# Edge rows scattered in columns of 124 rows instead of 128, with zero rows in pieces of many sizes

## The chip, the cores and the metric

The kernel runs on one core of a Trainium2 chip. The metric is the device time of one execution in microseconds (us). A core has five engines that run side by side: TensorE (PE; its weight loads are shown apart as PEld), VectorE (DVE), ScalarE (ACT), GpSimd (POOL) and SyncE (SP), and 16 DMA engines that move data between the DRAM (HBM) and the on-chip memory of 128 partitions.

## The reference

A graph layer. 206250 edges, sorted by destination, carry a row of 128 numbers each; the row of every edge is added to its source node (6250 nodes). The sums go with the node's features and a global row through a small MLP; the input is added back and each row is normed.

```python
edge_aggr = jnp.zeros((n, HIDDEN), dtype=x.dtype).at[row].add(edge_features)   # row = src
combined = jnp.concatenate([x, edge_aggr, global_expand], axis=-1) @ W_c + b_c
h = jax.nn.softplus(combined @ W1 + b1)
h = jax.nn.softplus(h @ W2 + b2)
return _layernorm(x + h @ W3 + b3)
```

## The kernel before, in words

The kernel first sorts the edge rows by their source node, in DRAM, and then sums what lies together. Nodes are taken in blocks of 128, so there are `NB` = 49 buckets. In the scratch tensor `bucketed` each bucket has room for a whole number of superchunks of 256 rows (`SC`; `NSC` = 854 in all). A row there has 129 numbers (516 bytes): the 128 of the edge and, last, the node's place in its block.

**Counting (lines 104 to 172).** The list of source nodes is laid out on 128 partitions: partition p holds the edges p x 1611 to p x 1611 + 1610 (`T` = 1611 columns), and one more column takes the 42 edges that are left (`R`), so `TC` = 1612. DVE turns node numbers into a bucket number (`block`) and a place within it (`low`), and then makes 49 passes over the columns (line 150), one for each bucket, which mark its edges (`in_block`) and count them. Two small matmuls and a scan give each bucket's start and each partition's first position (`base`).

**Zero rows (lines 174 to 190 and 216 to 218).** Behind the last edge of each bucket 256 zero rows are written, those that have no room there to a spare place behind all buckets. DVE works out the positions `pad_i`, and POOL writes them in two scatters of 128 rows for each bucket, 98 in all.

**Positions (lines 225 to 237).** In groups of 90 columns DVE runs, for each bucket, a scan (line 233) and a predicated copy (line 235), which give each edge its position; the group's positions become integers in `pos`.

**Row scatter (lines 239 to 253).** For each nine columns SP loads a tile `rows` (line 242) of 128 x 9 edge rows, ACT writes their `low` into the 129th place (line 245), and POOL issues nine indirect DMAs (line 210), one for each column, which send 128 rows each to the positions in that column of `pos`. The pool of `rows` has four buffers, and a load waits for the nine scatters that read its buffer last. POOL's queue holds the 98 zero scatters, then the 1612 row scatters, in this order; no two are held to be dependent on each other.

**Sums (lines 282 to 300).** When all scatters have landed, SP loads eight superchunks at a time (`chunks`); for each 128 rows DVE makes a one-hot matrix `hot` from the 129th number, TensorE multiplies it with the rows, and DVE adds the product to the block's part of `sums_t`.

**MLP (lines 321 to 362).** For 512 nodes at a time the three layers, the residual and the norm follow, and SP stores the rows.

Tile framework code puts in the waits; each engine works through its own queue in order.

## Time and profile before

| | us |
|---|---|
| time, median of two runs (3343.35 to 3343.64) | 3343.49 |
| span of the profiled execution, first to last instruction | 3156.7 |
| what lies around the span (median less span) | 186.8 |
| first scatter starts | 112.87 |
| first row scatter starts | 266.77 |
| last scatter starts, takes | 2319.15, 0.90 |
| first load of the sums issued | 2321.40 |

The profile is one execution; its span is the time between its first and its last instruction. The page gives no device time of its own for that execution, so the median of the runs stands for it, and the 186.8 us around the span are taken as fixed.

Busy time of the engines in the span: PE 716.9 us, PEld 527.9, DVE 1161.0, ACT 178.2, POOL 1695.3. A row of the groups names the line, the engine and the operation, what is written and read, how often, the busy time and mean length of one in ns, and the idle time of its engine just before it with what ended that idle time. "Issue" there means that the engine waited for nothing that the profile shows. Three more groups of the same page:

```profile
L233 DVE TENSOR_TENSOR_SCAN scan<-ones,scan,in_block 128x90 f32<-128x90 f32 (+1 forms) x833 | 323.1, 389 | 0.0
L235 DVE COPY_PREDICATED pos_f<-in_block,scan 128x90 f32<-128x90 uint8 (+1 forms) x882 | 200.0, 228 | 0.0
L150 DVE TENSOR_SCALAR_CACHE_REDUCE in_block<-block 128x1612 uint8<-128x1612 bf16 x49 | 85.9, 1821 | 0.0
```

The DMA issues give, after the count, the size of one and the median time from issue to landing:

```profile
rows<-in_edge_attr SPq DMA_DIRECT2D x179, 576.0 KB, 4.6
bucketed<-rows,pos POOLq DMA_INDIRECT x1612, 2.4
bucketed<-zeros,pad_i POOLq DMA_INDIRECT x98, 2.4
```

POOL's queue of DMAs (q0) shows 54720 packets and 113.01 MB, SP's queue (q1) 328812 packets and 228.93 MB.

### The profile page before, as it was taken

The numbers are of one execution on the slowest core, as the hardware profiler recorded it, in microseconds if no ns is written. First come the engines' busy times: TensorE is split into PE (matmuls) and PEld (weight loads), VectorE is DVE, ScalarE is ACT, GpSimd is POOL, SyncE is SP. The second block draws the span as 40 slices with busy tenths as digits, with TensorE's granted clock in tenths as the row PEclk, the third lists the DMA queues.
The fourth block names the chain that finished last, engine by engine and source line by source line (L and its number), as shares of the span: only waits on it lengthen the run. The fifth ranks groups of instructions, "written<-read, shape, count | busy, mean of one in ns | idle before, by whom it ended". The sixth has DMA issues, their size and how long they took to land. (4 is left out here: it accounts for less than half of the span.)

```text
span 3156.7 us, 18596 instructions
## 1 busy us (share of the span) xinstructions
PE 716.9 (23%) x3776; PEld 527.9 (17%) x3776; DVE 1161.0 (37%) x4793; ACT 178.2 (6%) x368; POOL 1695.3 (54%) x1720
## 2 busy tenths in 40 slices
PE   0000000000000000000000000000049999999885
PEld 0000000000000000000000000000037777777543
DVE  9999995000000000000000000000029999999644
ACT  0000000000000000000000000000000000000267
POOL 1577777777777777777777777777730000000000
PEclk9999999999999999999999999999999999999965
DMA  3012333333333333333333333333356565656200
GB/s 128 15 48 71 97 98 103 103 101 104 104 105 105 104 105 104 105 105 105 104 105 104 105 105 105 104 103 102 102 156 188 176 187 177 185 178 185 68 16 24
DMA packets 386717, 346.72 MB, mean 110 GB/s; under 512 B 33101, under 2 KB 355802, under 8 KB 386602
## 3 DMA queue, kind: packets, MB, share of 16 engines
q1 hardware_dynamic: 328812, 228.93, 25.8%
q0 software_dynamic: 54720, 113.01, 11.0%
q10 hardware_dynamic: 3070, 3.60, 0.4%
q14 instruction: 85, 0.70, 0.1%
q8 instruction: 30, 0.49, 0.1%
HBM read 222.83 MB, written 122.57 MB: 109 GB/s over the span
## 5 line engine op out<-in xcount | busy, mean ns | idle before, releaser
L210 POOL DMA_INDIRECT bucketed<-rows,pos x1612 | 1562.0, 969 | 491.6 <-issue 489.4
L297 PE MATMUL part<-hot,chunks 128*128 128x128 f32 x3416 | 569.9, 302 | 2273.1 <-DVE hot L295 2246.5
L295 DVE TENSOR_SCALAR hot<-iota_f,chunks 128x128 f32<-128x128 f32 x1708 | 406.7, 280 | 1818.5 <-DMA chunks<-bucketed 1812.8
L297 PEld LDWEIGHTS part<-hot,chunks 128*128 128x128 f32 x3416 | 448.2, 191 | 2394.1 <-issue 2213.6
L233 DVE TENSOR_TENSOR_SCAN scan<-ones,scan,in_block 128x90 f32<-128x90 f32 (+1 forms) x833 | 323.1, 389 | 0.0
L300 DVE TENSOR_TENSOR sums_t<-sums_t,part 128x128 f32 x854 | 245.4, 287 | 63.2 <-PE part L297 34.9
L235 DVE COPY_PREDICATED pos_f<-in_block,scan 128x90 f32<-128x90 uint8 (+1 forms) x882 | 200.0, 228 | 0.0
L210 POOL DMA_INDIRECT bucketed<-zeros,pad_i x98 | 124.0, 1266 | 132.5 <-DVE pos_f L235 103.3
L245 ACT COPY rows<-low 128x9 f32<-128x9 f32 x179 | 36.6, 206 | 2230.0 <-DMA bucketed<-rows,pos 2219.4
L150 DVE TENSOR_SCALAR_CACHE_REDUCE in_block<-block 128x1612 uint8<-128x1612 bf16 x49 | 85.9, 1821 | 0.0
L329 ACT ACTIVATE comb<-comb_ps,c_bias 128x512 f32<-128x512 f32 (+1 forms) x13 | 8.4, 646 | 617.4 <-PE comb_ps L326 617.4
L340 PE MATMUL y_ps<-w_sb,h 128*128 128x128 f32 (+1 forms) x98 | 33.2, 437 | 26.1 <-DVE h L313 25.6
L341 PE MATMUL y_ps<-b_row,ones 1*128 1x128 f32 (+1 forms) x98 | 35.6, 459 | 0.0
L340 PEld LDWEIGHTS y_ps<-w_sb,h 128*128 128x128 f32 (+1 forms) x98 | 24.6, 291 | 53.5 <-DVE h L313 36.4
L310 ACT ACT_TABLE_LOAD x26 | 33.4, 1283 | 0.5
L313 DVE TENSOR_TENSOR h<-h,away 128x512 f32<-128x512 f32 (+1 forms) x26 | 17.1, 656 | 37.5 <-ACT away L310 37.5
L318 PE MATMUL z_ps<-h,w_sb 128*128 128x512 f32 (+1 forms) x26 | 22.8, 976 | 9.3 <-DVE h L313 9.3
L154 PE MATMUL before_ps<-count,after 128*128 128x49 f32 x2 | 0.7, 432 | 106.7 <-DVE in_block L150 106.7
L342 DVE TENSOR_TENSOR y<-y_ps,x_sb 128x128 f32<-128x128 f32 (+1 forms) x49 | 13.8, 285 | 29.6 <-PE y_ps L341 29.6
L309 ACT ACT_TABLE_LOAD x19 | 24.4, 1283 | 0.3
L341 PEld LDWEIGHTS y_ps<-b_row,ones 1*128 1x128 f32 (+1 forms) x98 | 22.1, 279 | 9.9 <-issue 8.5
L312 DVE TENSOR_SCALAR h<-z_ps,cols 128x512 f32<-128x512 f32 (+1 forms) x26 | 18.2, 707 | 14.7 <-ACT away L308 14.7
(85 smaller groups left out, 284.8 us busy)
## 6 DMA issues: line engine op xcount, KB each, us to landing
chunks<-bucketed SPq DMA_DIRECT2D x106, 1032.0 KB, 5.3
rows<-in_edge_attr SPq DMA_DIRECT2D x179, 576.0 KB, 4.6
bucketed<-rows,pos POOLq DMA_INDIRECT x1612, 2.4
bucketed<-zeros SPq DMA_DIRECT2D x14, 451.5 KB, 8.7
out<-y SPq DMA_DIRECT2D x12, 256.0 KB, 2.2
bucketed<-zeros,pad_i POOLq DMA_INDIRECT x98, 2.4
src_i<-in_src SPq DMA_DIRECT2D x1, 805.5 KB
chunks<-bucketed SPq DMA_DIRECT2D x1, 774.0 KB
```

The lines of the kernel that those rows point to most:

```text
L150: nc.vector.tensor_scalar(in_block[:, b, :], block, float(b), None, op0=ALU.is_equal, op1=ALU.add, accum_out=count[:, b:b + 1])
L210: s = nc.gpsimd.indirect_dma_start(out=bucketed[:, :], out_offset=bass.IndirectOffsetOnAxis(ap=index, axis=0), in_=rows, in_offset=None)
L233: nc.vector.tensor_tensor_scan(scan[:, b, :n], ones[:, :n], in_block[:, b, g0:g1], first, op0=ALU.mult, op1=ALU.add)
L235: nc.vector.copy_predicated(pos_f[:, g0:g1], in_block[:, b, g0:g1], scan[:, b, :n])
L245: nc.scalar.copy(rows[:, :k, D:W], low[:, c0:c0 + k].unsqueeze(2))
L295: nc.vector.tensor_scalar(hot, iota_f, chunks[:, s, j, D:W], None, op0=ALU.is_equal)
L297: nc.tensor.matmul(part, chunks[:, s, j, :D], hot, start=(j == 0), stop=(j == SUB - 1))
L300: nc.vector.tensor_add(here, here, part)
L309: nc.scalar.activation(away[:, :w], away[:, :w], AF.Exp, scale=-1.0)
L310: nc.scalar.activation(away[:, :w], away[:, :w], AF.Ln, bias=ones[:, :1])
L340: nc.tensor.matmul(y_ps[:r, :], h2[:, q0:q0 + r], w_sb["w3"], start=True, stop=False)
L341: nc.tensor.matmul(y_ps[:r, :], ones[:1, :r], b3_row, start=False, stop=True)
```

## The change

The edges are laid out on `EP` = 124 partitions: `T` becomes 1663, `R` 38 and `TC` 1664. Every tile with an edge on each partition (`src_i`, `node`, `block`, `low`, `in_block`, `count`, `pos`, `scan`, `rows`) shrinks to 124 partitions, and a row scatter sends 124 rows. The load of a tile of nine columns is issued as two DMAs, of 112 and of 12 partitions. `rows` has three buffers instead of four.

The 256 zero rows behind a bucket are scattered in pieces whose sizes come from a table of eight entries, one after the other over the buckets. The pieces of a bucket lie a constant step apart, which POOL writes with one `iota` for each bucket. The positions take 8 columns for each bucket instead of 2, used or not, and `bucketed` has more spare rows. The rest of the diff removes comments.

```diff
+EP = 124
+PAD_SIZES = ((127, 127, 2), (122, 122, 12), (124, 124, 8), (112, 112, 32), (64,) * 4, (32,) * 8,
+             (128, 128), (96, 96, 64))
+PAD_MAX = 8
...
-    T, R = divmod(E, P)
+    T, R = divmod(E, EP)
...
-    bucketed = dram.tile([ROWS + NB * SUB * P, W], F32, name="bucketed")
+    bucketed = dram.tile([ROWS + NB * PAD_MAX * P, W], F32, name="bucketed")
...
-        rows_p = phase.enter_context(tc.tile_pool(name="rows", bufs=4))
+        rows_p = phase.enter_context(tc.tile_pool(name="rows", bufs=3))
...
-        in_block = keep.tile([P, NB, TC], U8, name="in_block")
+        in_block = keep.tile([EP, NB, TC], U8, name="in_block")
...
-        nc.gpsimd.iota(spare, pattern=[[SUB * P, NB], [P, SUB]], base=ROWS, channel_multiplier=1,
-                       allow_small_or_imprecise_dtypes=True)
+        nc.gpsimd.iota(spare, pattern=[[PAD_MAX * P, NB], [P, PAD_MAX]], base=ROWS,
+                       channel_multiplier=1, allow_small_or_imprecise_dtypes=True)
+        for b in range(NB):
+            size = PAD_SIZES[b % len(PAD_SIZES)][0]
+            nc.gpsimd.iota(pad_f[:, b, :], pattern=[[size, PAD_MAX]], base=0,
+                           channel_multiplier=1, allow_small_or_imprecise_dtypes=True)
         nc.vector.tensor_add(pad_end, start, total)
-        for k in range(SUB):
-            nc.vector.tensor_scalar(pad_f[:, :, k], pad_end, part_f, float(k * P),
-                                    op0=ALU.add, op1=ALU.add)
+        for k in range(PAD_MAX):
+            nc.vector.tensor_add(pad_f[:, :, k], pad_f[:, :, k], pad_end)
             nc.vector.scalar_tensor_tensor(over[:, :, k], end, float(SC), pad_f[:, :, k],
                                            op0=ALU.mult, op1=ALU.is_le)
...
         for b in range(NB):
-            for k in range(SUB):
-                scatter(zeros[:, :W], pad_i[:, b, k:k + 1])
+            for k, r in enumerate(PAD_SIZES[b % len(PAD_SIZES)]):
+                scatter(zeros[:r, :W], pad_i[:r, b, k:k + 1])
...
-                rows = rows_p.tile([P, LOAD_COLS, W], F32, name="rows")
-                nc.sync.dma_start(
-                    rows[:, :k, :D],
-                    edge_attr[:P * T, :].rearrange("(p t) d -> p t d", p=P)[:, c0:c0 + k, :])
+                rows = rows_p.tile([EP, LOAD_COLS, W], F32, name="rows")
+                of = edge_attr[:EP * T, :].rearrange("(p t) d -> p t d", p=EP)
+                for p0, p1 in ((0, 112), (112, EP)):
+                    nc.sync.dma_start(rows[p0:p1, :k, :D], of[p0:p1, c0:c0 + k, :])
```

More of the change, by code (lines that the diff above doesn't have):

```diff
@@ L100 @@
         scans = phase.enter_context(tc.tile_pool(name="scans", bufs=2))
-        rows_p = phase.enter_context(tc.tile_pool(name="rows", bufs=4))
+        rows_p = phase.enter_context(tc.tile_pool(name="rows", bufs=3))
         ps = phase.enter_context(tc.tile_pool(name="ps", bufs=1, space=PSUM))
-        src_i = keep.tile([P, TC], I32, name="src_i")
+        src_i = keep.tile([EP, TC], I32, name="src_i")
         if R:
             nc.vector.memset(src_i[:, T:TC], 0)
-        nc.sync.dma_start(src_i[:, :T], src[:P * T].rearrange("(p t) -> p t", p=P))
+        nc.sync.dma_start(src_i[:, :T], src[:EP * T].rearrange("(p t) -> p t", p=EP))
         if R:
-            nc.sync.dma_start(src_i[:R, T:TC], src[P * T:].rearrange("(p o) -> p o", o=1))
+            nc.sync.dma_start(src_i[:R, T:TC], src[EP * T:].rearrange("(p o) -> p o", o=1))
         ZR = 7
@@ L121 @@
             )
-        node = keep.tile([P, TC], F32, name="node", tag="t0")
-        wrap = keep.tile([P, TC], F32, name="wrap", tag="t1")
+        node = keep.tile([EP, TC], F32, name="node", tag="t0")
+        wrap = keep.tile([EP, TC], F32, name="wrap", tag="t1")
         nc.vector.tensor_copy(node, src_i)
@@ L131 @@
         nc.vector.tensor_add(src_i, node, wrap)
-        part_i = keep.tile([P, TC], I32, name="part_i", tag="t1")
-        block = keep.tile([P, TC], BF16, name="block")
+        part_i = keep.tile([EP, TC], I32, name="part_i", tag="t1")
+        block = keep.tile([EP, TC], BF16, name="block")
         nc.vector.tensor_scalar(part_i, src_i, 7, None, op0=ALU.arith_shift_right)
@@ L136 @@
         if R:
-            none = keep.tile([P, 1], F32, name="none")
-            nc.vector.tensor_scalar(none, part_f, R - 0.5, 128.0, op0=ALU.is_gt, op1=ALU.mult)
+            none = keep.tile([EP, 1], F32, name="none")
+            nc.vector.tensor_scalar(none, part_f[:EP], R - 0.5, 128.0, op0=ALU.is_gt, op1=ALU.mult)
             nc.vector.tensor_add(block[:, T:TC], block[:, T:TC], none)
-        low_i = keep.tile([P, TC], I32, name="low_i", tag="t0")
-        low = keep.tile([P, TC], F32, name="low")
+        low_i = keep.tile([EP, TC], I32, name="low_i", tag="t0")
+        low = keep.tile([EP, TC], F32, name="low")
         nc.vector.tensor_scalar(low_i, src_i, P - 1, None, op0=ALU.bitwise_and)
         nc.vector.tensor_copy(low, low_i)
-        in_block = keep.tile([P, NB, TC], U8, name="in_block")
-        count = keep.tile([P, NB], F32, name="count")
+        in_block = keep.tile([EP, NB, TC], U8, name="in_block")
+        count = keep.tile([EP, NB], F32, name="count")
         for b in range(NB):
@@ L153 @@
         before_ps = ps.tile([P, NB], F32, name="before_ps")
-        nc.tensor.matmul(before_ps, after, count, start=True, stop=True)
+        nc.tensor.matmul(before_ps, after[:EP, :], count, start=True, stop=True)
         total_ps = ps.tile([P, NB], F32, name="total_ps")
-        nc.tensor.matmul(total_ps, ones, count, start=True, stop=True)
+        nc.tensor.matmul(total_ps, ones[:EP, :], count, start=True, stop=True)
         total = keep.tile([P, NB], F32, name="total")
@@ L172 @@
         nc.vector.scalar_tensor_tensor(base, start, -1.0, before_ps, op0=ALU.add, op1=ALU.add)
-        pad_f = keep.tile([P, NB, SUB], F32, name="pad_f")
+        pad_f = keep.tile([P, NB, PAD_MAX], F32, name="pad_f")
         pad_end = keep.tile([P, NB], F32, name="pad_end")
-        over = keep.tile([P, NB, SUB], F32, name="over")
-        spare = keep.tile([P, NB, SUB], F32, name="spare")
-        pad_i = keep.tile([P, NB, SUB], I32, name="pad_i")
-        nc.gpsimd.iota(spare, pattern=[[SUB * P, NB], [P, SUB]], base=ROWS, channel_multiplier=1,
-                       allow_small_or_imprecise_dtypes=True)
+        over = keep.tile([P, NB, PAD_MAX], F32, name="over")
+        spare = keep.tile([P, NB, PAD_MAX], F32, name="spare")
+        pad_i = keep.tile([P, NB, PAD_MAX], I32, name="pad_i")
+        nc.gpsimd.iota(spare, pattern=[[PAD_MAX * P, NB], [P, PAD_MAX]], base=ROWS,
[4 more added lines that the diff above has]
+                           channel_multiplier=1, allow_small_or_imprecise_dtypes=True)
         nc.vector.tensor_add(pad_end, start, total)
-        for k in range(SUB):
-            nc.vector.tensor_scalar(pad_f[:, :, k], pad_end, part_f, float(k * P),
-                                    op0=ALU.add, op1=ALU.add)
+        for k in range(PAD_MAX):
+            nc.vector.tensor_add(pad_f[:, :, k], pad_f[:, :, k], pad_end)
             nc.vector.scalar_tensor_tensor(over[:, :, k], end, float(SC), pad_f[:, :, k],
@@ L216 @@
         for b in range(NB):
-            for k in range(SUB):
-                scatter(zeros[:, :W], pad_i[:, b, k:k + 1])
-        pos_f = keep.tile([P, TC], F32, name="pos_f", tag="t0")
+            for k, r in enumerate(PAD_SIZES[b % len(PAD_SIZES)]):
+                scatter(zeros[:r, :W], pad_i[:r, b, k:k + 1])
+        pos_f = keep.tile([EP, TC], F32, name="pos_f", tag="t0")
         nc.vector.memset(pos_f, 0.0)
-        pos = keep.tile([P, TC], I32, name="pos", tag="t1")
+        pos = keep.tile([EP, TC], I32, name="pos", tag="t1")
         last = None
@@ L229 @@
             n = g1 - g0
-            scan = scans.tile([P, NB, GROUP_COLS + 1], F32, name="scan")
+            scan = scans.tile([EP, NB, GROUP_COLS + 1], F32, name="scan")
             for b in range(NB):
-                first = base[:, b:b + 1] if last is None else last[0][:, b, last[1] - 1:last[1]]
-                nc.vector.tensor_tensor_scan(scan[:, b, :n], ones[:, :n], in_block[:, b, g0:g1],
+                first = base[:EP, b:b + 1] if last is None else last[0][:, b, last[1] - 1:last[1]]
+                nc.vector.tensor_tensor_scan(scan[:, b, :n], ones[:EP, :n], in_block[:, b, g0:g1],
                                              first, op0=ALU.mult, op1=ALU.add)
@@ L249 @@
         if R:
-            rows = rows_p.tile([P, LOAD_COLS, W], F32, name="rows")
-            nc.sync.dma_start(rows[:R, 0, :D], edge_attr[P * T:, :])
+            rows = rows_p.tile([EP, LOAD_COLS, W], F32, name="rows")
+            nc.sync.dma_start(rows[:R, 0, :D], edge_attr[EP * T:, :])
             nc.scalar.copy(rows[:R, 0, D:W], low[:R, T:TC])
```

## The prediction

> **What bounds the kernel now.** I read the engine totals and the slices first, then the time by stage, then the groups of line L210, then the timeline around the end of the scatters. The printed chain of waits follows only the last stage (its longest pieces start at 2717 us and its shares add up to some 15%), so the first two thirds must be read from the engines.

> ```profile
> DVE  9999995000000000000000000000029999999644
> ACT  0000000000000000000000000000000000000267
> POOL 1577777777777777777777777777730000000000
> ```

> Each digit is a fortieth of the span. POOL works from the second slice to the thirtieth while DVE is done by the seventh and PE is idle; the rest of the kernel begins when POOL ends. The same by stage (columns: us, then busy time and instructions of PE, PEld, DVE, ACT, POOL, then clock, DMA share, GB/s):

> ```profile
> 0.00:112.87 112.87, 3.89 (x9) 1.42 (x9) 104.98 (x139) 1.79 (x5) 9.26 (x10) 1.00 0.27 89
> 112.87:266.77 153.90, 1.23 (x4) 0.50 (x2) 153.68 (x671) 0.00 (x0) 124.03 (x98) 1.00 0.13 42
> 266.77:519.00 252.23, 0.00 (x0) 0.00 (x0) 252.15 (x1111) 4.13 (x20) 195.96 (x185) 1.00 0.34 96
> 519.00:2320.05 1801.05, 0.00 (x0) 0.00 (x0) 0.00 (x0) 32.16 (x156) 1366.07 (x1427) 1.00 0.36 103
> 2320.05:3156.70 836.65, 711.77 (x3765) 526.00 (x3765) 650.21 (x2875) 140.09 (x187) 0.00 (x0) 0.91 0.47 143
> ```

> Stages: counting on DVE; 98 pad scatters; row scatters beside DVE's scans; row scatters alone; sums and MLP. In the fourth, 1427 scatters take 1801.05 us: 1.2621 us each. In the third it is 252.23/185 = 1.3634, so 0.101 more beside the scans. DMA engines are a third busy. What fills 1.26 us:

> ```profile
> L210 POOL DMA_INDIRECT bucketed<-rows,pos x1612 | 1562.0, 969 | 491.6 <-issue 489.4
> L210 POOL DMA_INDIRECT bucketed<-zeros,pad_i x98 | 124.0, 1266 | 132.5 <-DVE pos_f L235 103.3
> ```

> The row scatters wait for nothing but issue (0.304 us each); their data and buffers are there. One pad scatter took 20.85 us, once. The kernel pays **a fixed toll per scatter instruction**. How that toll depends on rows has one witness, the last scatter, of 42 rows:

> ```profile
> 2317.89 0.95 POOL L210 DMA_INDIRECT bucketed<-rows,pos  x1 [0.30 <-issue]
> 2319.15 0.90 POOL L210 DMA_INDIRECT bucketed<-rows,pos  x1 [0.31 <-issue]
> ```

> In nanoseconds 896 against 957: a third of the rows costs 94% of the time. The trace's packet records add how they are spread: a 128-row scatter is sixteen packets of 4128 B (8 rows of 516 B on each engine); the 42-row one is fourteen of 1548 B (3 rows) and two of 12 B.

> [...] 0.96 us spans, landing 2.4 us after issue. [...] The 42-row witness fits both, for 42/14 = 3 and 42/16 rounds up to 3. Whether an indirect scatter follows the divisor rule no record here shows; that is the crux. [...] the trace shows 1.07 us spans beside the scans and 0.96 without.

> **The change, part by part,** against the profiled span of 3156.7 us; the median of 3343.49 lies 186.8 above it, carried over unchanged.

> The model for one scatter: 16 engines get as many slots as the fullest has rows. 8 slots cost 957 ns, 3 cost 896, so 12.2 ns a slot on a base of 860, plus the gap of 304. I choose the rounded-up share: 124 rows are then 8 slots, as 128 are, because the two 12-byte packets look like three dummy entries of 4 B for each engine without rows, and a writer that fills all sixteen anyway needs no divisor.

> 1. *Prologue, on the path.* The 49 counting passes are spaced 1.75 us and grow by 1664/1612: +2.8. The casts before them, some 13 us: +0.4. Pad arithmetic: 12 more small ops at about 0.17 us (the present four span 0.7) = +2.0; three ops of 392 instead of 98 elements, at one more ns per element: +0.9. Sum +6. If the scheduler slips a scan of 0.39 us between these ops, as it does now, twice that. The 49 new iotas on POOL cost 0.24 to 1.12 us (the rows of the present ones), 12 to 55 us, and sit ahead of the first scatter; POOL is idle from 9.9 to 112.87 us, which hides them, and would show them if more than 90 us.
> 2. *Pads.* Per eight buckets 3+3+3+3+4+8+2+3 = 29 pieces, so 177 for 49 buckets instead of 98, with the same 12544 zero rows. Beside scans one costs (153.90 - 19.9)/98 = 1.367, the one-off stall of 19.9 taken out. Slots under my choice: 131 per eight buckets, 803 in all, 613 fewer than 177 x 8: 177 x 1.367 - 7.5 + 19.9 = 254.3 against 153.9, **+100**.
> 3. *Rows.* 1663 columns of 124 and one of 38, instead of 1611 and one of 42. Scans need 19 groups, not 18: 49 pairs at 0.462 us put DVE's end at 519 + 6 + 22.6 = 548, hidden behind POOL throughout. Pads end at 373, so 128 scatters run beside scans: 128 x 1.3634 + 1535 x 1.2621 + 1.2 = 2113 against 2053.3, **+60**.
> 4. *Loads.* Two DMAs a tile of nine columns, 185 tiles: 370 issues of 0.37 us instead of 179 on SP's queue, which otherwise waits. Each of the two, and the ACT copy, waits for the nine scatters that free the buffer; only later tiles stand behind them. With three buffers a freed one is needed after 2 x 9 x 1.26 = 22.7 us, less 2.4 to land, and a load lands in 4.6: at nothing, as long as cover of some 15 us stays. [...] Bounds: nothing to 0.37 us once.
> 5. *Unchanged:* 854 superchunks are read and summed, 836.65 us. Larger scratch in DRAM is only allocated.

> Sum: 6 + 100 + 60 = +166, span 3323, time **3510**. If a slot costs nothing or twice as much the pads move by 8; with item 1's bound and doubt over contention, 3480 to 3550.

> **The rivals.**
> *A, divisor rule with every slot paid.* 124 rows go to 4 engines, 31 slots: 957 + 23 x 12.2 = 1238 ns, pitch 1.543 alone. Pad slots: 255 for the 127s, 123 for the 122s, 63 for the 124s, 16 in each other bucket, 521 per eight, 3381 in all: 1965 more than 177 x 8, +24, pads 286, +132. Rows: 87 x 1.644 + 1576 x 1.543 + 1.4 = 2576, +522. Time 3343 + 6 + 132 + 522 = **4003**. For it: [...] the 12-byte packets show slots filled on idle engines. [...] If contention too goes by slots (0.101 for 8), the 170 or so contended scatters add up to 50, and the long pads 20.
> *B, the set of engines sets the toll.* The 61 ns of the witness would be two engines fewer, 30.5 each. With the divisor rule 124 rows save 12 x 30.5 = 366 ns, pitch 0.896; pads use 2140 engine shares instead of 2832: 241 us, +87; rows 188 x 0.997 + 1475 x 0.896 = 1509, -544. Time **2892**, faster. It decides from the point where a 124-row scatter is written in under 0.817 us: 166 - 1663 x 0.140 = -67. Against: even the idle two have packets [...].
> *C, four fixed engines fill up.* A packet of 8 rows takes 194 ns, so 31 rows 0.752 us, and a column's share of the loads is 72 packets of 32 ns over nine columns, 0.256: 1.01 us, under the pitch. At 32 ns a row it is 1.25, still level: the transfers stay hidden and the time is that of the case above.
> *D, the change doesn't reach the toll:* if pad pieces were cheap (half of 1.367), pads fall by 121: 3343 + 6 - 21 + 60 = 3388, no difference. The 42-row witness at 94% speaks against.

> **How the numbers follow.** About 2%, 67 us, separates a difference from none. My choice, with C inside it, has 0.56; A 0.27, of it 0.05 above 4060; a cost between or beyond, from a writer less even than the model, 0.07, 0.02 of it high; B 0.07; D 0.03. Slower 0.90, same 0.03, faster 0.07. The likeliest time is 3510. Its own 3480 to 3550 holds just over half, so the range must reach A: 3470 to 4060 leaves out B, D and the high tails, 0.17.

> **What would show it.** Row scatters 1664, pads 177; the 124-row span at 0.95 to 0.96 us with packets of 4128 B (my choice), or near 1.24 with packets of some 16 kB (A), or under 0.82 (B). Pad spans by size: 127 rows as 128 here, 2.4 us in A. First scatter near 119 us, DVE done near 548, POOL done near 2486, then 836 us as before. Wrong would be a scatter that waits for DMA rather than issue, or an idle POOL at a tile's border (item 4).

## The result, and the profile after

The changed kernel takes 3951.64 us, the kernel before 3343.49 in the same comparison: ratio 1.1813, interval 1.1778 to 1.1847. In later comparisons the kernel before took 3347 us once, on chip 10, and 3159 to 3163 three times, on chips 1, 4 and 1 (the chip of the first comparison is not on record), while the changed kernel took 3952 in the first comparison, 3952 beside 3159 and 3955 beside 3163; so the ratio is 1.25 (1.2507, interval 1.2482 to 1.2532) where the kernel before is at 3159.

The time of the changed kernel's profiled execution, 3953.97, lies 1.8 us above its span of 3952.2. The profile of before (span 3156.7) therefore belongs to an execution of some 3158 us, and the 187 us that I took to lie around its span don't exist. The two traces differ by 795.5 us of span.

The slices of the page after (engines, fortieths of the span):

```profile
DVE  8988990000000000000000000000000299999944
ACT  0000000000000000000000000000000000000067
POOL 1677888888888888888888888888888300000000
```

The shape is the same, POOL's stage is longer and its busy share higher, eight tenths for seven. By stage, in the columns of the table before (prologue; pads; rows beside scans; rows alone; the rest):

```profile
0.00:125.51 125.51, 5.13 (x11) 1.91 (x11) 110.53 (x152) 1.69 (x4) 12.46 (x59) 1.00 0.23 75
125.51:405.29 279.78, 0.00 (x0) 0.00 (x0) 235.67 (x997) 0.00 (x0) 225.83 (x178) 1.00 0.10 24
405.29:610.00 204.71, 0.00 (x0) 0.00 (x0) 195.90 (x883) 2.69 (x13) 166.65 (x126) 1.00 0.33 77
610.00:3109.83 2499.83, 0.00 (x0) 0.00 (x0) 0.00 (x0) 35.05 (x170) 2031.38 (x1539) 1.00 0.34 79
3109.83:3952.20 842.37, 715.65 (x3765) 528.50 (x3765) 650.95 (x2875) 139.95 (x187) 0.00 (x0) 0.90 0.46 143
```

Stage by stage that is +12.6 for the prologue, +125.9 for the pads, +651.3 for the rows (204.71 + 2499.83 against 252.23 + 1801.05) and +5.7 for the rest. The groups of the scatters, and the last two of them in POOL's timeline:

```profile
L219 POOL DMA_INDIRECT bucketed<-rows,pos x1664 | 2198.0, 1321 | 506.8 <-issue 505.6
L219 POOL DMA_INDIRECT bucketed<-zeros,pad_i x177 | 225.8, 1276 | 166.1 <-DVE pos_f L244 112.4
```

```profile
3107.09 1.32 POOL L219 DMA_INDIRECT bucketed<-rows,pos  x1 [0.30 <-issue]
3108.72 1.11 POOL L219 DMA_INDIRECT bucketed<-rows,pos  x1 [0.30 <-issue]
```

The scatters still wait for issue alone, 0.304 us each; the span of one has grown from 957 to 1321 ns although it carries four rows fewer. The last one, of 38 rows, takes 1109 ns where 42 rows took 896. The packet records say why. They name no engine, but the data of a 124-row scatter move in four chains, each of three packets of 4128 B and one of 3612, one packet starting as the one before it ends: 31 rows on each of four engines. Beside the sixteen of 4 B that every scatter has, the rest are packets of 32 and 28 bytes, that is 8 and 7 entries of 4 B, as many as give the other twelve engines 31 entries each. The queue's line counts them: 144048 packets where 54720 were.

```profile
q0 software_dynamic: 144048, 115.66, 13.0%
```

So the divisor rule of rival A holds for these scatters: the packets lie on as many engines as the largest divisor of the rows up to 16 (124 = 4 x 31; 38 = 2 x 19, although 19 divides it too; 122 = 2 x 61; 127 on one; 32, 64, 96, 112 and 128 on sixteen). And every engine's list is filled to the length of the fullest: with 124 rows the packets of 32 and 28 bytes make twelve lists of 31 entries, with 127 rows fifteen of 127. The pad pieces show the cost by size. POOL's timeline over the start of the second round of the table (127, 127, 2; 122, 122; columns: start, us):

```profile
189.10 2.57 POOL L219 DMA_INDIRECT bucketed<-zeros,pad_i  x1 [0.31 <-issue]
191.97 2.58 POOL L219 DMA_INDIRECT bucketed<-zeros,pad_i  x1 [0.30 <-issue]
194.86 0.87 POOL L219 DMA_INDIRECT bucketed<-zeros,pad_i  x1 [0.30 <-issue]
196.03 1.83 POOL L219 DMA_INDIRECT bucketed<-zeros,pad_i  x1 [0.30 <-issue]
198.17 1.73 POOL L219 DMA_INDIRECT bucketed<-zeros,pad_i  x1 [0.31 <-issue]
```

127 rows, on one engine, take 2.6 us; 128 rows take 0.97 in the pads' stage (median of twelve).

### The profile page after: what moved, and what is told of

It is laid out like the page before. It is cut to its first block, busy times and chain, and to the rows that moved or that the text cites. A ratio compares the mean times of both kernels' runs of the same rounds, so it can differ in the third digit from the quotient of the medians.

```text
span 3952.2 us, 19326 instructions
## 1 busy us (share of the span) xinstructions
PE 720.8 (18%) x3776; PEld 530.4 (13%) x3776; DVE 1193.1 (30%) x4904; ACT 179.4 (5%) x374; POOL 2436.3 (62%) x1900
## 3 DMA queue, kind: packets, MB, share of 16 engines
q0 software_dynamic: 144048, 115.66, 13.0%
## 5 line engine op out<-in xcount | busy, mean ns | idle before, releaser
L219 POOL DMA_INDIRECT bucketed<-rows,pos x1664 | 2198.0, 1321 | 506.8 <-issue 505.6
L242 DVE TENSOR_TENSOR_SCAN scan<-ones,scan,in_block 124x90 f32<-124x90 f32 (+1 forms) x882 | 343.9, 394 | 1.6 <-DVE pos_f L244 1.1
L219 POOL DMA_INDIRECT bucketed<-zeros,pad_i x177 | 225.8, 1276 | 166.1 <-DVE pos_f L244 112.4
L244 DVE COPY_PREDICATED pos_f<-in_block,scan 124x90 f32<-124x90 uint8 (+1 forms) x931 | 214.0, 231 | 39.8 <-DVE scan L242 20.5
L254 ACT COPY rows<-low 124x9 f32<-124x9 f32 x185 | 38.0, 206 | 3016.9 <-DMA bucketed<-rows,pos 3007.0
L156 DVE TENSOR_SCALAR_CACHE_REDUCE in_block<-block 124x1664 uint8<-124x1664 bf16 x49 | 88.5, 1879 | 0.0
```

Source lines behind the costliest of these rows:

```text
L156: nc.vector.tensor_scalar(in_block[:, b, :], block, float(b), None, op0=ALU.is_equal, op1=ALU.add, accum_out=count[:, b:b + 1])
L219: s = nc.gpsimd.indirect_dma_start(out=bucketed[:, :], out_offset=bass.IndirectOffsetOnAxis(ap=index, axis=0), in_=rows, in_offset=None)
L242: nc.vector.tensor_tensor_scan(scan[:, b, :n], ones[:EP, :n], in_block[:, b, g0:g1], first, op0=ALU.mult, op1=ALU.add)
L244: nc.vector.copy_predicated(pos_f[:, g0:g1], in_block[:, b, g0:g1], scan[:, b, :n])
L254: nc.scalar.copy(rows[:, :k, D:W], low[:, c0:c0 + k].unsqueeze(2))
```

## The experiments

**The kernel before, again.**

> The kernel before, unchanged, profiled again. The changed kernel's time lies 2 us above its span (3953.97 against 3952.2), the kernel before's median lies 187 above the span of its profile. Theory 1: one profile simply caught a quicker execution than the timed ones; then this span is near 3341, its time less 2, and a scatter of 128 rows is paced some 0.11 us slower (near 1.37) for most of the stage. Theory 2: 187 us do lie around the span in this kernel; then the span is 3157 again and the pace 1.262.

3160.42 us, span 3156.8: ratio 1.0002 (0.9993 to 1.001). Neither theory as I put it: the span is 3157 again, but so is the time. Nothing lies around the span; it was the first comparison's 3343 that differed.

**The two parts of the change, one at a time.** First the columns of 124 with the old pads:

```diff
-PAD_SIZES = ((127, 127, 2), (122, 122, 12), ...
-PAD_MAX = 8
+PAD_SIZES = ((128, 128),)
+PAD_MAX = 2
```

> Edges in columns of 124 rows, zero rows in two pieces of 128 as before. Slot theory (124 rows go to 4 engines, 31 slots each, every slot paid on all sixteen): row scatters stay at 1.32 us, and the time falls only by what the pad pieces cost, some 125 us, to 3825. Count theory (a scatter costs the same whatever its rows, and the many pads are the loss): 52 more scatters at 1.26 to 1.37, some 3415.

3807.35 us beside 3159.13 (ratio 1.2036, 1.2015 to 1.2056): slot theory. Then the table of pads with `EP = 128`:

> Columns of 128 rows, zero rows in pieces from the table. Slot theory: row scatters as before, pads 280 us instead of 154, prologue 10 more: some 3343 + 135 = 3480, and pieces of 127, 122 and 124 rows at 2.57, 1.72 and 1.32 us while 128, 96, 64 and 32 stay under 1.1. Count theory, all pieces alike at 1.37: 79 x 1.37 = 108, 3455, and no piece stands out. If the pads carried the loss: 3900.

3285.95 us beside the same 3159.13 (1.0386, 1.0369 to 1.0404). The +135 was expected of a base of 3343; the base here was lower and the rise is +127. Count theory's +112 is too little, and pieces do stand out: 127, 122 and 124 rows take 2.62, 1.73 and 1.32 us (medians). The groups of the row scatters in these two kernels:

```profile
L218 POOL DMA_INDIRECT bucketed<-rows,pos x1664 | 2178.1, 1309 | 507.0 <-issue 506.4 <-DVE scan L241 0.3 <-DMA bucketed<-rows,pos 0.3
```

```profile
L219 POOL DMA_INDIRECT bucketed<-rows,pos x1612 | 1551.9, 963 | 491.6 <-issue 491.3 <-DVE pos_f L244 0.3
```

The slow scatter goes with the 124 rows and not with the pads. The parts add up to 648 + 127 = 775; the whole, run beside 3159.2, gave +793:

> The changed kernel as it is, beside the kernel before on the chip where that took 3159. Its two parts done alone cost +648 and +127 there, so slot theory: 3159 + 775 = 3934, up to 3952 if nothing but the kernel before had moved between the two comparisons. If everything had been slower by 187 us in the first comparison: 3765.

3952.49 us. The 18 us between 775 and 793 are about what the row scatters differ by: they are busy for 2196.6 us here (1320 ns each) and for 2178.1 with the old pads (1309). What makes those 11 ns stays open.

**Another number that sixteen doesn't divide.** `EP = 126`, plain pads:

> Columns of 126 rows: 126 = 14 x 9, so 14 engines with 9 slots, 1637 columns. Slot theory: the span of a scatter is 0.97 to 0.98 us, one slot above 128 rows, and the time is up by 25 x 1.27 + 1637 x 0.012 = 52 us, near 3395. A rule that any number of rows other than a multiple of 16 takes a slow way: 1.2 us or more, 3750. Rounded-up share on 16 engines (8 slots): 3375, and 16 packets with data instead of 14.

3222.71 us beside 3159.13 (1.0196, 1.0178 to 1.0213), +64 where 52 were expected. The median span of a row scatter beyond the scans is 974 ns, one slot above 957, and for each scatter the packet records show fourteen packets of 4128 B and fourteen of 516, nine rows on each of fourteen engines. Not being a multiple of sixteen costs 17 ns a scatter here; what counts is the slots, 9 for 126 rows (974 ns) and 31 for 124 (1309).

**124 edges to a column, 128 rows to a scatter.**

```diff
+        nc.gpsimd.iota(pos, pattern=[[4, TC]], base=ROWS + NB * PAD_MAX * P - EP, channel_multiplier=1)
...
-                rows = rows_p.tile([EP, LOAD_COLS, W], F32, name="rows")
+                rows = rows_p.tile([P, LOAD_COLS, W], F32, name="rows")
...
+                nc.sync.dma_start(rows[EP:, :k, :D], of[:P - EP, c0:c0 + k, :])
```

> Still 124 edges to a column and 1664 columns, but each scatter sends 128 rows: four more rows that nobody reads, to places behind all buckets. Slot theory: 16 engines and 8 slots again, 0.957 us a scatter, 3159 + 52 x 1.26 + 10 = 3235. If the loss lay in the layout by 124 (loads, copies, positions on 124 partitions): 3800 as with 124 rows.

3238.82 us beside 3159.2 (1.0248, 1.0228 to 1.0269). Sending four useless rows along saves 569 us against the 3807 of the same columns with 124 rows. It is also what my prediction's choice stands for, eight slots in 1664 scatters, and it comes to +80, of which 66 are the 52 further scatters.

**A ladder of sizes.** 128-row columns and another table: 31 x 8 + 8; 62 x 4 + 8; 93, 93, 70; 124, 124, 8; 51 x 5 + 2; 119, 119, 18; 85 x 3 + 2; 126, 126, 4. The framework put 37 of the 225 pieces ahead of the row scatters all the same; the others ran with DVE idle.

> Columns of 128 rows; zero rows from another table, scattered after all row scatters, when DVE is idle. Slot theory, span set by rows / engines and not by rows: pieces of 31, 62, 93 and 124 rows (31 slots on 1, 2, 3, 4 engines) all at 1.30 to 1.32 us; 51, 85 and 119 rows (17 slots on 3, 5, 7) alike, near 1.10; 126 (9 slots) 0.97; 70 (5) 0.91; 18 (2) and 8 (1) 0.87. If rows or engines were paid: 31 rows well under 124, by half or more of what lies above 0.87.

3360.88 us, in one execution; the spans of the pieces are what counts here. POOL's timeline, one round of the table from its second piece on (31 rows; 8; 62; 8; 93; 70; 124; 8; 51):

```profile
2253.73 1.27 POOL L219 DMA_INDIRECT bucketed<-zeros,pad_i  x1 [0.31 <-issue]
...
2264.73 0.87 POOL L219 DMA_INDIRECT bucketed<-zeros,pad_i  x1 [0.30 <-issue]
2265.91 1.29 POOL L219 DMA_INDIRECT bucketed<-zeros,pad_i  x1 [0.30 <-issue]
...
2273.43 1.31 POOL L219 DMA_INDIRECT bucketed<-zeros,pad_i  x1 [0.30 <-issue]
2275.04 1.30 POOL L219 DMA_INDIRECT bucketed<-zeros,pad_i  x1 [0.30 <-issue]
2276.65 0.93 POOL L219 DMA_INDIRECT bucketed<-zeros,pad_i  x1 [0.30 <-issue]
2277.88 1.32 POOL L219 DMA_INDIRECT bucketed<-zeros,pad_i  x1 [0.30 <-issue]
...
2282.31 1.10 POOL L219 DMA_INDIRECT bucketed<-zeros,pad_i  x1 [0.30 <-issue]
```

Medians over the trace, with engines x slots:

| rows | engines x slots | ns | | rows | engines x slots | ns |
|---|---|---|---|---|---|---|
| 8 | 8 x 1 | 875 | | 85 | 5 x 17 | 1080 |
| 18 | 9 x 2 | 883 | | 119 | 7 x 17 | 1080 |
| 70 | 14 x 5 | 926 | | 31 | 1 x 31 | 1266 |
| 126 | 14 x 9 | 984 | | 62 | 2 x 31 | 1284 |
| 51 | 3 x 17 | 1081 | | 124 | 4 x 31 | 1323 |

51, 85 and 119 rows cost the same to a nanosecond, and 31 rows on one engine nearly what 124 on four do (93 on three: 1309). Rows and engines cost nothing between 3 x 17 and 7 x 17, and 57 ns in all between 1 x 31 and 4 x 31. Slots are what is paid: counted from a base of some 860 ns (estimated from 957 ns at 8 slots and 896 at 3), and from five slots up, 13 to 15 ns each in this table, 12 for the 128 rows of a column (957 ns) and 13.5 for the 127 slots of a 127-row piece (2570 ns).

**The loads.** One DMA of 124 partitions instead of 112 + 12:

> Columns of 124 rows and plain pads, but each tile of nine columns loaded by one DMA of 124 partitions instead of 112 + 12. By the divisor rule the load too then runs on 4 engines: 31 x 9 = 279 packets of 512 B at 32 ns on each, 8.9 us, against a tile's 9 x 1.61 = 14.5 us of scatters: the landing goes from some 5 us to 10 and the time stays at 3807. If loads were near the bound (the split being what keeps them hidden): scatters waiting on DMA and over 3850.

3801.95 us, 1.2028 of the kernel before (1.1999 to 1.2057), where the split load took 3807 beside the same 3159. The 1116 packets of a tile now take 10.6 us from first to last instead of 3.8, which fits the divisor rule on SP's queue too (8.9 us was the estimate for four engines); and no scatter waits for them. POOL's waits in this kernel:

```profile
POOL bucketed L218 <- issue: 521.5, 1712, 0.3
POOL bucketed L218 <- DVE pos_f L243: 109.8, 3, 109.2
POOL bucketed L218 <- DMA bucketed<-rows,pos: 14.3, 47, 0.3
```

The 14.3 us in the last line are 47 times the usual 0.3 of issue, not waits of their own.

**Fewer scatters.** If the toll is per instruction, the pads are better written by someone else:

```diff
-        for b in range(NB):
-            for k in range(SUB):
-                scatter(zeros[:, :W], pad_i[:, b, k:k + 1])
...
+                z = nc.sync.dma_start(
+                    bucketed[bass.ds(at[b], SC), :].rearrange("(p j) c -> p (j c)", p=P),
+                    zeros[:, :SUB * W])
```

> The kernel before, but the 256 zero rows behind each bucket are written by 49 plain DMAs on SP's queue, from an address in a register, instead of 98 scatters on POOL; what runs over into the next bucket is overwritten by its rows, which are scattered after all zeros have landed. If the toll of POOL's scatters is the bound of this stage, the pads' 154 us shrink to what the first group of positions takes, some 25 to 30 us (POOL waits for it near 136 us in the span), and the time is near 3159 - 130 + a few = 3035. If SP's 49 issues and landings are serial at 2 us and more each, the row scatters begin near 230 and the time is 3120 or no better than before.

3232.56 us beside 3346.83 (0.9656, 0.964 to 0.9672), on chip 10. All three kernels once more, together, on chip 1:

> The kernel before once more. It took 3343 in the first comparison, 3159 in two others, 3347 in the last. Where it takes 3345: if DVE's scans are what stretch (as in the run with the zeros on SP, where a predicated copy waited 1.5 us and more at a time and DVE worked until 2250), its DVE is busy over the whole scatter stage and scatters of 128 rows take about 1.07 us on average instead of 0.957; a slower POOL alone would show 1.07 with DVE done near 519. Where it takes 3159: DVE done near 519, 0.957.

> Zeros by 49 plain DMAs on SP, once more, for the other kind of comparison. If the kernel before takes 3159 here, this one takes 3159 - 115 = 3045, with DVE done near 520; if before takes 3345, again 3232.

> The changed kernel once more: 3950 in either kind of comparison, since it took 3952 beside both 3343 and 3159; a ratio of 1.18 where before takes 3345 and 1.25 where it takes 3159. If it had its own slow kind: over 4100.

Here the kernel before took 3162.7, this version 3059.34 (0.9665, 0.9643 to 0.9688) and the changed kernel 3955.49 (1.2488, 1.2458 to 1.2518). The version beats the kernel before in both comparisons. Its issues on SP and its first row scatter, in the run at 3059:

```profile
112.74 35.70 SPq L208 DMA_DIRECT2D bucketed<-zeros  x49
```

```profile
153.52 1.18 POOL L197 DMA_INDIRECT bucketed<-rows,pos  x1 [144.69 <-DVE pos_f L229]
```

The rows begin at 153.5 us instead of 266.8. I had expected some 139, and the first group of positions is ready at 135; the other 14 us are the zeros' issue, which ends at 148, and landing.

The run at 3232 shows what is different on chip 10. DVE's slices there, and two of its waits (us in total, times, longest; "remote" means that the trace names no instruction that ended the wait):

```profile
DVE  9952222222222222222222222110018999999644
```

```profile
DVE pos_f L229 <- remote: 1074.2, 476, 4.3
DVE pos_f L229 <- issue: 397.0, 146, 4.4
```

The predicated copies wait up to 4.4 us each, DVE's scans stretch over nearly the whole scatter stage instead of its first fifth, and a row scatter takes 1065 ns on average. There is no trace of the kernel before at 3343, but the changed kernel's trace from that comparison bears the same mark, which its two later traces, beside 3159 and 3163, lack:

```profile
DVE pos_f L244 <- remote: 16.5, 10, 2.2
```

Its copies wait 39.8 us in all there, every time beside a pad piece of 127, 128, 96, 64 or 32 rows; of the 437 copies beside the 124-row scatters none waits. That fits a changed kernel that takes 3952 to 3955 in every comparison. That the 184 us of the kernel before come from such waits is likely, then, but still not shown. Why they appear in some comparisons only stays open; chip 10 served in one comparison, too few to put it down to the chip.

## Why the prediction was wrong

**The step that failed is the choice in the model for one scatter**: "I choose the rounded-up share: 124 rows are then 8 slots, as 128 are". They are 31, so a row scatter takes 1321 ns instead of 957, and the rows cost +651 us instead of +60. My reading of the two 12-byte packets as three dummy entries each was right, as the 32- and 28-byte packets confirm. The inference from it, that a writer which fills all sixteen lists "needs no divisor", was not: the lists are filled and the divisor still decides how long they are (31 entries for 124 rows, 9 for 126). The 42-row witness could not tell the two apart, since 42 has the divisor 14, and that A deserved the smaller chance, 0.27 against 0.56, was an estimate of mine that no record of before bore out.

**Rival A was the mechanism**, and its time of 4003 is near by luck, through two errors that offset each other. Its span would have been 3817, 135 short of 3952; the 187 carried over for what "lies around the span" filled the gap. The term that was mis-sized is the slot: 12.2 ns, read between 3 and 8 slots, against (1321 - 957)/23 = 15.8 between 8 and 31. That is 3.6 x 23 x 1663 = 138 us. Its pads were right: 286 against 279.8. The measured time lies within my range of 3470 to 4060 only because the range was stretched to reach A; the likeliest time, 3510, stood for the wrong mechanism.

Item by item:
- *The bound and the toll:* right that the cost of each scatter instruction on POOL sets the stage, waits are for issue (505.6 of 506.8 us) and transfers stay hidden; but the toll is fixed only in part, the base of some 860 ns and the 304 of issue.
- *Prologue, +6:* measured +12.6. Missed was the load of `src_i`, which the change also lays on 124 partitions and doesn't split: DVE's first cast starts at 13.2 us instead of 6.1 (at 6.3 in the run with the table of pads and 128 partitions). The pads' arithmetic was as thought; the iotas were hidden as thought, and took 4.3 us for all 49 instead of 12 to 55.
- *Pads, +100:* +126, for the slots of the pieces of 127, 122 and 124 rows.
- *Rows, +60:* +651. The run with 128 rows to a scatter shows that the count of scatters alone gives about what I had.
- *Scans beside scatters, 0.101 us each:* not for 124 rows. Their pace is 1.634 us beside the scans and 1.625 without, in the two later traces 1.629 and 1.630 beside them. DVE's scans, which I had ending near 548 us, end at 551 and 550 in those two and at 601 in the first, where its copies wait.
- *Loads at nothing:* right, with even more cover than needed, as the unsplit load shows. In two parts a tile of 124 partitions is loaded in 3.8 us, in one in 10.6; the kernel takes no longer with one (3802 us for 3807).
- *Rest unchanged:* +5.7; the cause stays open.
- *B* fell: with engines going from 16 to 4 the span rose, and it differs by 57 ns between one engine and four at equal slots. *C* held, nothing waits for a transfer, although a scatter lands 3.7 us after its issue with columns of 124 rows and 6.0 with the unsplit load, instead of 2.4 (medians). *D* fell: a piece of 2 or 8 rows costs 875 ns.

## What to carry to other kernels

Price the scatters on POOL by their number first (here some 860 ns of base, an estimate from the spans of 8 and 3 slots, and 304 of issue for each) and then by the fullest engine of each: in these runs the engines were the largest divisor of the rows that is at most 16, and rows over divisor the slots, at 12 to 15 ns for each (rows of 516 B). Where that divisor is small, try a few useless rows sent to a place that nobody reads (124 to 128 saved 569 us here), and keep rows whose place is known as one run away from POOL altogether (3059 us for 3163 here). And where one witness fits two rules, look for a second one before choosing.
